# Batched VectorE operations for the token places, rows and weights of eight small experts in a perceiver layer

## The chip, the core and the metric

The kernel runs on one core of a Trainium2 chip, in float32 throughout its large products. A core has five engines that run their own instruction queues: PE (TensorE, matrix products), DVE (VectorE), ACT (ScalarE), POOL (GpSimd) and SP (SyncE, which here only issues transfers). The metric is device time in microseconds (us), the median of three executions: 758.45 us before the change (758.18 to 758.95).

## What is computed

One layer of a perceiver over 256 tokens of width 512: cross-attention with a sigmoid over a context of 25,088 rows, causal self-attention, and a mixture of experts. Only the last part matters here:

```python
logits = x @ gate_w                          # 256 tokens, 64 experts
w, idx = top_k(softmax(logits), 8)           # w divided by its sum
pos = (place of the token among those that chose the same expert)
slot = minimum(pos, CAPACITY)                # CAPACITY = 256
buf[e_flat, slot] = x[tok]
gu_e = einsum('ech,ehf->ecf', buf, expert_gate_up_w)
act = silu(gu_e[..., :I]) * gu_e[..., I:]
out_e = einsum('eci,eih->ech', act, expert_down_w)
y = out_e[e_flat, slot] * w_flat[:, None]
return y.sum(over the 8 choices) + shared    # shared: a gated expert that every token uses
```

## The kernel before

Up to about 560 us the kernel computes the cross-attention (lines L336 to L593 in the profile's largest groups), then the self-attention. The expert part begins near 611 us. The shared expert is cut in four pieces, `("s", 0)` to `("s", 3)`. The 64 experts are sorted by how many tokens chose them. The seven largest, `("e", 0)` to `("e", 6)`, are computed for all 256 tokens. The next eight (numbers 7 to 14, `FEW` = 8) are small: for these only the tokens that chose them are gathered, into four rounds of 128 slots. A round holds quarters of 32 slots: round 0 has three quarters of expert 9 and one of expert 10, round 1 one quarter each of experts 11 to 14, round 2 three of expert 8 and one of expert 7, round 3 four of expert 7.

The function `run` (L1474) goes through the pieces `("s", 0)` to `("s", 3)`. For each it calls `gate_up`: a product on PE (L1263), a sigmoid on ACT (L1289), two products on VectorE (L1290, L1291), and a scaling `weigh` on VectorE (L1300), after which VectorE adds four sums `s_s` (L1364) and POOL four sums `t_s` (L1364) for a down product in seven block products (`seven`, L1380). After piece i it calls the step of the dictionary `between`: `counted` after piece 0, `load_first` after 1, `ranked_tokens` after 2, `seated` after 3. The seven products of a piece stand on PE's queue behind the gate and up products of the next piece.

`ranked_tokens` brings the routing weights into the sorted order (`wso`) and finds for each token its `rank` among those that chose each of the eight small experts, -1 where it did not (L1638, L1646). `rank` has 128 partitions (tokens) by 2 halves of the tokens by 8 experts. `seated` then

- writes `places_of`, one 0/1 matrix of tokens by slots for each half and round: for each of the two halves of the tokens and each of nine ranges of slots one VectorE comparison of the slot numbers `slot_sb` with one column of `rank` (L1663, 18 operations of 32, 96 or 128 columns),
- multiplies it on PE with the token numbers (`token`, L1673, 8 small products), turns the result into integers (`token_i`, L1681), and has POOL issue four indirect gathers of the tokens' rows (`few_rows`, L1683),
- computes for each small expert the row from which a token will later fetch its result (`row`, L1697 and L1700), and the weight that it fetches with (`fetched_w`, L1703): three operations of 128x2 elements for each of eight experts, 24 in all, after a `memset` of `row` (L1692),
- turns `row` into integers (`row_of_token`, L1706), and clears the weights of fetched tokens in `wso` (L1709, eight operations).

The VectorE and POOL instructions of `seated` carry no fixed place; a scheduler puts them among those of `gate_up`. In the program before, 13 of the comparisons stand ahead of L1290 of piece 3 on VectorE's queue, the other five comparisons and 25 of the small operations between L1290 and L1291, and L1706 and one more between L1291 and L1300. On PE the order is: gate and up products of piece 3, the seven products of piece 2, the eight `token` products, the seven products of piece 3, then the first large expert.

The row `fn` of normalised tokens, from which the gathers read, is written by VectorE at L282 in two halves, transposed by PE (L298), and stored by POOL (`rows_of_tokens`, L1181).

Of the kernel before, what the change touches and what calls it, by code (L numbers as in the profile page):

```python
# [9 lines left out]
F32 = mybir.dt.float32  # L10
BF16 = mybir.dt.bfloat16
AF = mybir.ActivationFunctionType
ALU = mybir.AluOpType
AX = mybir.AxisListType

P = 128
# [6 lines left out]
def tile_perceiver_layer(  # L23
# [25 lines left out]
    nc = tc.nc  # L49
# [10 lines left out]
    NT = T // P  # L60
# [175 lines left out]
    slot_sb = const.tile([P, T], F32, tag="slot", name="slot_sb")  # L236
# [284 lines left out]
    for i in range(2):  # L521
        t = cpool.tile([P, NT_SUMS, WIDTH + 2], F32, tag=f"T{i}", name=f"T_{i}", bufs=1)
# [94 lines left out]
    for t in range(NT):  # L617
        for c in range(ND):
            at = (c % 2) * T + t * P
# [82 lines left out]
    for line in RESULTS.strip().splitlines():  # L702
        to, x_, op, y_ = line.split()
        a_, b_, o_ = result(x_), result(y_), result(to)
        n = widths[to] = min(widths[x_], widths[y_])
        assert to not in ("c01", "c11") or n == WIDTH
        if to[0] == "c" and to[2] != "1":
            n = WIDTH - 2
# [74 lines left out]
    def banks(name):  # L783
        return pairs.tile([P, 2, 512], F32, tag="two", name=name)
# [7 lines left out]
    def bank(name):  # L792
        turns[1] += 1
        return apart(name) if turns[1] % 4 == 0 else among_three(name)
# [3 lines left out]
    for t in range(NT):  # L798
# [14 lines left out]
    WHOLE = 7  # L813
    QUARTER = P // 4
# [7 lines left out]
    NR = len(ROUNDS)  # L822

    STORED = ((0,), (1,), (2, 3))
    QUARTERS = {
        k: sum(n for part in ROUNDS for of, n in part if of == k)
        for k in sorted({of for part in ROUNDS for of, _ in part})
    }
    FEW = len(QUARTERS)
# [363 lines left out]
    few = ctx.enter_context(tc.tile_pool(name="few", bufs=1))  # L1193
# [197 lines left out]
    def add_seven():  # L1391
# [18 lines left out]
    first, second = (  # L1410
        [pair[:, half, :] for half in range(2)]
        for pair in (banks("ph_first"), banks("ph_second"))
    )
# [146 lines left out]
    places_of = few.tile([P, NT, NR, P], BF16, tag="places_of", name="places_of")  # L1560
# [6 lines left out]
    fetched_w = few.tile([P, NT, FEW], F32, tag="fetched_w", name="fetched_w")  # L1567
# [40 lines left out]
    def slots_of_round(r):  # L1608

        first = 0  # L1610
        for k, n in ROUNDS[r]:
            ahead = sum(m for part in ROUNDS[:r] for of, m in part if of == k) * QUARTER
            yield k, first, n * QUARTER, ahead
            first += n * QUARTER

    rank = few.tile([P, NT, FEW], F32, tag="rank", name="rank")
    w = wso[:, :, WHOLE : WHOLE + FEW]

# [26 lines left out]
        )  # L1645
        nc.vector.tensor_scalar(rank, rank, 1.0, None, ALU.subtract)  # L1646

    def first_row(k):
        for rounds in STORED:
            for i, r in enumerate(rounds):  # L1650
                for of, first, _, ahead in slots_of_round(r):
                    if of == k:
                        assert ahead == 0
                        return i * P + first

    def seated():


        for t in range(NT):
            for r in range(NR):  # L1660
                for k, first, n, ahead in slots_of_round(r):
                    i = k - WHOLE
                    nc.vector.tensor_scalar(  # L1663
                        places_of[:, t, r, first : first + n],
                        slot_sb[:, ahead : ahead + n],
                        rank[:, t, i : i + 1],
                        None,
                        ALU.is_equal,
                    )
        token = bank("token")[:, 0:NR]  # L1670
        for r in range(NR):
            for t in range(NT):
                nc.tensor.matmul(  # L1673
                    token[:, r : r + 1],
                    lhsT=places_of[:, t, r, :],
                    rhs=tokens_sb[:, t : t + 1],
                    start=(t == 0),
                    stop=(t == NT - 1),
                )
        token_i = few.tile([P, NR], mybir.dt.int32, tag="token_i", name="token_i")  # L1680
        nc.vector.tensor_copy(token_i, token)  # L1681
        for r in range(NR):
            nc.gpsimd.indirect_dma_start(  # L1683
                out=few_rows[:, r, :],
                out_offset=None,
                in_=rows_of_tokens[:, :],
                in_offset=bass.IndirectOffsetOnAxis(ap=token_i[:, r : r + 1], axis=0),
            )


        row = few.tile([P, NT, FEW], F32, tag="row", name="row")
        nc.vector.memset(row, 0.0)  # L1692
        for k, n in QUARTERS.items():
                i = k - WHOLE
                first = first_row(k)
                n *= QUARTER
                nc.vector.tensor_scalar(  # L1697
                    row[:, :, i], rank[:, :, i], 0.0, n - 1.0, ALU.max, ALU.min
                )
                nc.vector.tensor_scalar(  # L1700
                    row[:, :, i], row[:, :, i], float(first), None, ALU.add
                )
                nc.vector.scalar_tensor_tensor(  # L1703
                    fetched_w[:, :, i], rank[:, :, i], float(n), w[:, :, i], ALU.is_lt, ALU.mult
                )
        nc.vector.tensor_copy(row_of_token, row)  # L1706
        for k, n in QUARTERS.items():
            i = k - WHOLE
            nc.vector.scalar_tensor_tensor(  # L1709
                w[:, :, i], rank[:, :, i], float(n * QUARTER), w[:, :, i], ALU.is_ge, ALU.mult  # L1710
            )

    run(
        [("s", k) for k in range(NS)],
# [259 lines left out]
```

## Time and profile before

| | before |
|---|---|
| median of three executions | 758.45 us |
| profiled execution, whole | 758.16 us |
| its span | 756.0 us |
| PE busy | 748.9 us (99%) |
| VectorE busy | 574.9 us (76%) |
| POOL busy | 208.9 us (28%) |
| L1663, 18 operations | duration 224 to 808 ns, median 229 |
| L1697, L1700, L1703, L1709, 32 operations | 145 to 155 ns each |
| granted TensorE clock | 1.0 |

The span is the time from the first to the last recorded work of the profiled execution; 2.2 us of its whole time lie around it. In the profile, an answer on the chain of waits goes back from the last instruction to what released it, and shows which engine held up the end at each moment. A timeline shows the instructions of an engine with start, length, and what ended the idle time before them. Consecutive VectorE operations overlap in these records: an operation of 150 ns may follow another after 70 ns, so the distance from start to start, and not the duration, says what an operation costs in a row of them.

### The profile page before, as it was taken

Reading aid. Unit: us, or ns where it says so; the run is one execution under the profiler, and the core shown is the slowest. Engines: PE = TensorE matmul, PEld = TensorE weight load, DVE = VectorE, ACT = ScalarE, POOL = GpSimd, SP = SyncE. Lnnn points to the kernel's source line nnn. Section 1 sums busy time; section 2 is a strip of 40 time slices with the busy share of each in tenths; the row PEclk is TensorE's granted clock in tenths of the full one; section 3 lists DMA queues with packets and bytes.
Section 4 is the critical chain, followed back from the end, with each engine's and each line's share of the span. In section 5 each row is a group of like instructions: output and inputs, shape, how many; then the busy total and the mean of one; then the engine's idle time right before and its main releaser. Section 6 shows DMA issues by size and latency. Waiting matters only on the chain.

```text
span 756.0 us, 12474 instructions
## 1 busy us (share of the span) xinstructions
PE 748.9 (99%) x4046; PEld 614.3 (81%) x4046; DVE 574.9 (76%) x1682; ACT 200.7 (27%) x484; POOL 208.9 (28%) x378
## 2 busy tenths in 40 slices
PE   8999999999999999999999999999999999999998
PEld 6888888888888888888888888888977578876775
DVE  6988887887888788788888878878677569542465
ACT  4222222222222222222222222222244530001110
POOL 3222222232232222223222222322213305440461
PEclk9999999999999999999999999999999999999999
DMA  9999989997887887787788778774060018998552
GB/s 248 262 234 253 276 217 304 251 214 196 206 189 176 216 192 172 201 200 183 187 210 189 170 211 196 177 198 95 1 219 33 2 38 283 388 339 320 174 176 71
DMA packets 156147, 148.64 MB, mean 197 GB/s; under 512 B 8310, under 2 KB 113923, under 8 KB 156080
## 3 DMA queue, kind: packets, MB, share of 16 engines
q1 hardware_dynamic: 153168, 140.28, 71.3%
q0 software_dynamic: 2240, 7.02, 2.8%
q8 instruction: 33, 0.54, 0.3%
q10 hardware_dynamic: 672, 0.52, 0.2%
q14 instruction: 34, 0.28, 0.1%
HBM read 145.63 MB, written 2.16 MB: 195 GB/s over the span
## 4 chain that ended last, share of the span: by engine, by line
PE 97%; DVE 2%; DMA 0%; ACT 0%; issue 0%
PE xacc L593 38%; PE pk L372 22%; PE pz L392 11%; PE ph_e L1263 7%; PE seven L1380 3%; PE pa L914 2%; PE pw L983 2%; PE ph_few L1745 2%; PE ph_s L1263 1%; PE po_few L1776 1%; PE ph_first L1263 1%; PE ph_second L1263 1%; PE pd_last L1448 1%; PE ptp L1065 1%; PE ps L1009 1%; PE py L757 1%
## 5 line engine op out<-in xcount | busy, mean ns | idle before, releaser
L593 PE MATMUL xacc<-T,S 128*128 128x172 f32 (+2 forms) x912 | 185.5, 308 | 0.0
L372 PE MATMUL pk<-cT,wkT_sb 128*128 128x384 f32 x512 | 175.5, 486 | 0.0
L593 PEld LDWEIGHTS xacc<-T,S 128*128 128x128 f32 x912 | 152.6, 190 | 20.1
L372 PEld LDWEIGHTS pk<-cT,wkT_sb 128*128 128x128 f32 x512 | 97.1, 190 | 54.4
L560 POOL TENSOR_TENSOR T<-ctx 128x172 f32<-128x172 f32 x65 | 32.3, 496 | 386.1 <-PE xacc L593 375.5
L336 DVE STREAM_TRANSPOSE cT<-quarters 128x1536 f32<-128x1536 f32 x64 | 113.2, 1769 | 0.5 <-issue 0.5
L560 DVE TENSOR_TENSOR T<-ctx 128x172 f32<-128x172 f32 (+1 forms) x262 | 113.4, 433 | 0.0
L560 DVE TENSOR_TENSOR S<-zT 128x128 f32<-128x128 f32 x196 | 56.2, 287 | 70.9 <-ACT zT L401 70.9
L392 PE MATMUL pz<-qT,kT 128*128 128x256 f32 x392 | 106.1, 379 | 0.0
L401 ACT ACTIVATE zT<-pz 128x256 f32<-128x256 f32 (+1 forms) x131 | 64.2, 490 | 113.7 <-PE pz L392 113.7
L593 PE MATMUL xacc<-T,zT 128*128 128x173 f32 (+1 forms) x396 | 89.9, 308 | 0.0
L593 PE MATMUL xacc<-ctx,S 128*128 128x172 f32 x392 | 78.5, 309 | 0.0
L383 ACT ACTIVATE kT<-pk,bk 128x384 f32<-128x384 f32 (+2 forms) x68 | 38.5, 568 | 146.9 <-PE pk L372 146.9
L570 ACT COPY T<-ctx 128x170 f32<-128x170 f32 (+1 forms) x130 | 43.2, 334 | 124.9 <-PE xacc L593 123.5
L560 DVE TENSOR_TENSOR S<-zT,S 128x128 f32<-128x128 f32 x325 | 76.0, 283 | 0.0
L560 POOL TENSOR_TENSOR T<-ctx,T 128x170 f32<-128x170 f32 (+1 forms) x130 | 72.4, 576 | 0.0
L560 DVE TENSOR_TENSOR T<-ctx,T 128x172 f32<-128x172 f32 x195 | 65.4, 360 | 8.2 <-PE xacc L593 1.5
L392 PEld LDWEIGHTS pz<-qT,kT 128*128 128x128 f32 x392 | 68.5, 190 | 3.8 <-ACT kT L383 0.2
L593 PEld LDWEIGHTS xacc<-T,zT 128*128 128x128 f32 x396 | 66.4, 190 | 0.3
L593 PEld LDWEIGHTS xacc<-ctx,S 128*128 128x128 f32 x392 | 62.8, 190 | 0.1
L593 PE MATMUL xacc<-ctx,zT 128*128 128x170 f32 (+1 forms) x264 | 59.5, 307 | 0.0
L1263 PE MATMUL ph_e<-fT,gu 128*128 128x256 f32 x224 | 50.3, 381 | 0.0
(308 smaller groups left out, 793.9 us busy)
## 6 DMA issues: line engine op xcount, KB each, us to landing
ctx<-in_context SPq DMA_DIRECT2D x65, 768.0 KB, 5.3
quarters<-in_context SPq DMA_DIRECT2D x256, 192.0 KB, 6.5
gu<-in_e_gate_up SPq DMA_DIRECT2D x12, 1024.0 KB, 7.9
gu_s<-in_s_gate_up SPq DMA_DIRECT2D x8, 512.0 KB, 5.9
dn<-in_e_down SPq DMA_DIRECT2D x7, 512.0 KB, 6.6
a_wqT<-in_a_wqT SPq DMA_DIRECT2D x4, 512.0 KB, 10.0
a_wout<-in_a_woutT SPq DMA_DIRECT2D x1, 2048.0 KB, 11.6
dn_s<-in_s_down SPq DMA_DIRECT2D x4, 512.0 KB, 8.0
```

Source lines behind the costliest of these rows:

```text
L336: in_turn(nc.vector.transpose(new_turned(g), q.rearrange("p b (c r) -> p c b r", r=R)))
L372: nc.tensor.matmul(pk, lhsT=w[:, c, :], rhs=cT[:, c, 0 : n // R, :].rearrange("p b r -> p (b r)"), start=(c == 0), stop=(c == ND - 1),)
L383: in_turn(nc.scalar.activation(kT[:, lo:hi], pk[:, lo:hi], AF.Identity, bias=bk_sb))
L392: nc.tensor.matmul(pz[:, i * T : (i + 1) * T], lhsT=kT[:, at : at + P], rhs=qT, start=True, stop=True,)
L401: nc.scalar.activation(zT[:, blocks[0] : blocks[-1] + 1, :].rearrange("p j t -> p (j t)"), pz[:, 0 : len(blocks) * T], AF.Sigmoid, scale=1 ...
L560: in_turn(f(o_, a_, b_))
L570: in_turn(nc.scalar.copy(named[to][:, 0:n], named[x_][:, 0:n]))
L593: nc.tensor.matmul(banks_of_products[i][:, cols], lhsT=named[lhs], rhs=named[rhs][:, 0:n],  start=i not in opened, stop=(g == G - 1 and last),
L914: nc.tensor.matmul(pa[:, 0 : hi - lo], lhsT=a_wqT_sb[:, c, e * P : (e + 1) * P], rhs=anT[:, c, lo:hi], start=(c == 0), stop=(c == ND - 1),)
L983: nc.tensor.matmul(pw[t], lhsT=oT[:, e, t * P : (t + 1) * P], rhs=a_wout_sb[:, e, :], start=(e == 0), stop=(e == NE - 1),)
L1263: nc.tensor.matmul(ph[:, f * T + lo : f * T + hi], lhsT=gu[:, c, col : col + P], rhs=fT[:, c, lo:hi], start=(c == 0), stop=(c == ND - 1),)
L1380: nc.tensor.matmul(product_of_seven(nm), lhsT=block(n, hT, dn, s_, t_, lhs), rhs=block(n, hT, dn, s_, t_, rhs),  start=(n == SEVEN[0] and ...
```

## The change

The 18 comparisons become eight. A list `places` holds the ranges of slots, where neighbouring one-quarter experts with neighbouring numbers are one entry: for each half of the tokens one comparison of 96 columns (expert 9), one `tensor_tensor` of 160 columns for experts 10 to 14 together (`slot_sb` and `rank` both broadcast), one of 96 (expert 8) and one of 160 (expert 7, over the border of two rounds). The 24 operations for `row` and `fetched_w`, the `memset` and the eight for `wso` become five operations over all eight experts; with the cast they are six. Three constants for each expert are taken from a new small tile `numbers` (128 partitions by 3 by 8), which POOL fills with 24 `memset` operations of 128x1 elements.

In the built program the instructions stand thus. On POOL the 24 memsets lie between the two stores of `rows_of_tokens` (L1181), and the first of them waits for the last reads of the memory that `numbers` takes over (VectorE's L1173 for the second half of the tokens, and PE's L983). On VectorE all eight comparisons, then the two operations of `row` and the cast, stand ahead of L1290 of piece 3; the last three operations stand between L1290 and L1291; none are between L1291 and L1300. `token_i` stands behind the four sums `s_s` of piece 3. The order on PE, ACT and SP is as before. The tiles of the same memory pool that follow `numbers` lie 96 bytes further on.

```diff
+    place_of, places = {}, []
+    for r in range(NR):
+        for k, within, n, ahead in slots_of_round(r):
+            at = r * P + within - ahead
+            assert place_of.setdefault(k, at) == at
+            if ahead:
+                continue
+            if places and QUARTERS[k] == 1:
+                k0, many, at0 = places[-1]
+                if QUARTERS[k0] == 1 and (k, at) == (k0 + many, at0 + many * QUARTER):
+                    places[-1] = (k0, many + 1, at0)
+                    continue
+            places.append((k, 1, at))
+
+    numbers = few.tile([P, 3, FEW], F32, tag="numbers", name="numbers")
+    for k, n in QUARTERS.items():
+        row_0 = min(rs[0] for rs in STORED if place_of[k] // P in rs) * P
+        for i, value in enumerate((n * QUARTER, n * QUARTER - 1, place_of[k] - row_0)):
+            nc.gpsimd.memset(numbers[:, i, k - WHOLE : k - WHOLE + 1], float(value))
+
+    def of_expert(i):
+        return numbers[:, i, :].unsqueeze(1).to_broadcast([P, NT, FEW])
...
     def seated():
+        flat = places_of.rearrange("p t r s -> p t (r s)")
         for t in range(NT):
-            for r in range(NR):
-                for k, first, n, ahead in slots_of_round(r):
-                    i = k - WHOLE
+            for k, many, at in places:
+                n = QUARTERS[k] * QUARTER
+                i = k - WHOLE
+                if many == 1:
                     nc.vector.tensor_scalar(
-                        places_of[:, t, r, first : first + n],
-                        slot_sb[:, ahead : ahead + n],
+                        flat[:, t, at : at + n],
+                        slot_sb[:, 0:n],
                         rank[:, t, i : i + 1],
                         None,
                         ALU.is_equal,
                     )
+                else:
+                    nc.vector.tensor_tensor(
+                        flat[:, t, at : at + many * n].rearrange("p (e s) -> p e s", e=many),
+                        slot_sb[:, 0:n].unsqueeze(1).to_broadcast([P, many, n]),
+                        rank[:, t, i : i + many].unsqueeze(2).to_broadcast([P, many, n]),
+                        ALU.is_equal,
+                    )
...
-        nc.vector.memset(row, 0.0)
-        for k, n in QUARTERS.items():
-                i = k - WHOLE
-                first = first_row(k)
-                n *= QUARTER
-                nc.vector.tensor_scalar(
-                    row[:, :, i], rank[:, :, i], 0.0, n - 1.0, ALU.max, ALU.min
-                )
-                nc.vector.tensor_scalar(
-                    row[:, :, i], row[:, :, i], float(first), None, ALU.add
-                )
-                nc.vector.scalar_tensor_tensor(
-                    fetched_w[:, :, i], rank[:, :, i], float(n), w[:, :, i], ALU.is_lt, ALU.mult
-                )
+        nc.vector.scalar_tensor_tensor(row, rank, 0.0, of_expert(1), ALU.max, ALU.min)
+        nc.vector.tensor_add(row, row, of_expert(2))
         nc.vector.tensor_copy(row_of_token, row)
-        for k, n in QUARTERS.items():
-            i = k - WHOLE
-            nc.vector.scalar_tensor_tensor(
-                w[:, :, i], rank[:, :, i], float(n * QUARTER), w[:, :, i], ALU.is_ge, ALU.mult
-            )
+        nc.vector.tensor_tensor(row, rank, of_expert(0), ALU.is_lt)
+        nc.vector.tensor_mul(fetched_w, row, w)
+        nc.vector.tensor_sub(w, w, fetched_w)
```

More of the change, by code (lines that the diff above doesn't have):

```diff
@@ L1646, in ranked_tokens @@
         nc.vector.tensor_scalar(rank, rank, 1.0, None, ALU.subtract)
[L1648 to L1654, printed above, removed]
     def seated():
+        flat = places_of.rearrange("p t r s -> p t (r s)")
         for t in range(NT):
-            for r in range(NR):
-                for k, first, n, ahead in slots_of_round(r):
-                    i = k - WHOLE
+            for k, many, at in places:
+                n = QUARTERS[k] * QUARTER
+                i = k - WHOLE
+                if many == 1:
                     nc.vector.tensor_scalar(
-                        places_of[:, t, r, first : first + n],
-                        slot_sb[:, ahead : ahead + n],
+                        flat[:, t, at : at + n],
+                        slot_sb[:, 0:n],
                         rank[:, t, i : i + 1],
                         None,
+                        ALU.is_equal,
[5 more added lines that the diff above has]
+                        rank[:, t, i : i + many].unsqueeze(2).to_broadcast([P, many, n]),
                         ALU.is_equal,
```

## The prediction

> **What bounds the kernel now.** I read the page first: PE is busy 748.9 us of 756.0, and the chain that ended last lies on PE for 97%. So VectorE's many operations cost nothing except where PE stands still for them, and the first question is where it does. The answer on PE's waits, over the whole span, has four rows (who waited for whom, total us, times, longest):
>
> ```profile
> PE pi L210 <- DVE idle_sb L97: 1.5, 1, 1.5
> PE seven L1380 <- DVE hT_s L1300: 0.7, 1, 0.7
> PE pt_xn L621 <- DVE xn L610: 0.6, 1, 0.6
> PE pa L914 <- ACT aq L928: 0.2, 1, 0.2
> ```
>
> Only the second lies in the changed stage. The chain of waits between 636 and 660 us (start, us, what) shows how it comes about:
>
> ```profile
> 644.34 0.07 PE pn L1631 x3
> ...
> 644.43 0.19 DVE rank L1638
> ...
> 644.64 0.66 DVE rank L1646
> ...
> 645.32 3.73 DVE places_of L1663 x13
> 649.05 0.59 DVE hT_s L1290
> 649.65 0.81 DVE places_of L1663 x5
> ...
> 652.22 0.60 DVE hT_s L1291
> 652.82 0.08 DVE row_of_token L1706
> 652.90 0.07 DVE wso L1709
> 652.97 0.61 DVE hT_s L1300
> 653.58 0.04 issue
> 653.62 3.29 PE seven L1380 x14
> ```
>
> From 644.43 to 653.62 the chain is VectorE's alone; it is 9 us long, but PE works beside nearly all of it. A table of busy time for that stretch (window, its length, PE, PEld, DVE, ACT and POOL busy, clock, DMA share, GB/s) says how much:
>
> ```profile
> 644.60:653.62 9.02, 8.28 (x46) 7.14 (x45) 8.95 (x52) 0.60 (x1) 2.76 (x4) 1.00 1.05 386
> ```
>
> VectorE is full (8.95 of 9.02) and PE misses 9.02 - 8.28 = **0.74 us**. That is the whole prize of this stage, whatever number of VectorE operations goes away: PE's timeline has the eight token products start at 652.54 and end 0.34 later, at 652.88, and the next seven products at 653.62.
>
> **The eight comparisons.** Before, 18 of them take 3.73 + 0.81 = 4.54 us of the chain. Part of this is POOL: its four sums `t_s` run at 644.53, 645.34, 646.02 and 646.71, the last until 647.44, and in that time VectorE gets only one operation through for each of POOL's (one of 96 columns from 645.32 lasts 0.81, one of 32 from 646.05 lasts 0.73, where the median is 229 ns). After: three operations (96, 160, 96) pass in that time as three passed before, and five are left at 647.4. Ten operations and the step to L1290 took 647.39 to 648.97 before, 0.158 each; the widest forms cost more, so I take 0.2 each: 648.4. The `tensor_tensor` of 160 columns is not in the trace of before. Its lower end is one comparison's 0.16; above, `s_s<-hT_s` of 128x128 from SBUF stands 0.20 apart (two in 0.48, the second lasting 0.28), and 32 more columns add about 0.03: 0.23. If it is held for a whole sum of POOL it costs 0.73, twice: 1.5. I take 0.23, the row of the same operation.
>
> **The six operations on 128x16.** Before, 25 small ones stood between L1290 and L1291 (650.38 to 652.14, 1.76 us, 0.07 apart because they alternate between experts) and two more between L1291 and L1300 (0.15). After, each operation reads what the one before it wrote. The row for that is L1638 to L1646, 644.43 to 644.64: 0.21 apart. Three of them before L1290: 648.4 + 0.63 = 649.0. L1290 takes 0.60: 649.6. Three more: 650.3. L1291 (its product on PE ends at 649.68, so nothing holds it) 0.60, L1300 0.61 and its 0.04: **651.5**. PE is through with the token products at 652.88. So VectorE comes some 1.3 us ahead of PE, and the gap closes even if one `tensor_tensor` is held for a full sum of POOL. What is late next is PE itself.
>
> **The rest of the edit.** The memset of `row` (L1692, 72 ns at 615.13) goes; VectorE waits 0.20 for ACT right behind it, which hides it: nothing. `token_i` stood at 654.73 and can now follow the token products near 653.1, so POOL's four gathers begin some 1.6 us earlier. They were through by 667, and PE reads `few_rows` at 673.4: nothing. The eight clearings of `wso` are read by nothing before the end: nothing. The sums `t_s` of piece 3 end at 647.44 and PE needs them at 654: a delay by the wider VectorE operations is covered sixfold.
>
> After 653.62 PE waits for no one by the table of waits, so 0.74 us at this place should reach the end in full, if no transfer is late. The DMA engines are full from 644 to 673 (share 1.05), so I looked for the nearest arrival. The weights of the second large expert are issued at 644.42 and take 7.9 us in the median, 10.9 at most: 655.3, read at about 664. Those of the third: 654.25 and 665.2, read at 674.0. Eight us of cover against 0.74. SP's later issues wait for PE to free buffers and move with it.
>
> **POOL's 24 memsets** are the one thing added. They wait for VectorE's L1173, which ends at 614.09, and stand ahead of POOL's second store of `rows_of_tokens` (616.66), whose rows are gathered 38 us later: as a delay of POOL this is nothing. But VectorE is then on the path to `fn`, and PE has almost no cover there:
>
> ```profile
> 0.28 0.10 POOL L1959 MEMSET const-float32-1.0<- 128x1 f32 x1
> 0.31 0.11 POOL L1959 MEMSET const-bfloat16-1.0<- 128x1 bf16 x1
> ...
> 615.64 0.72 DVE L282 TENSOR_SCALAR fn<-x,mv_f,rs_f 128x256 f32<-128x256 f32 x2
> ...
> 616.43 0.25 PEld L298 LDWEIGHTS pt_fn_behind<-ident,fn 128*128 128x128 f32 x2
> ```
>
> `fn` ends at 616.36 and PE loads it at 616.43: cover 0.07. The row for a memset of 128x1 on POOL is the start of the kernel: 0.10 to 0.12 long, but 0.03 apart. By it 24 take 24 x 0.03 + 0.1 = 0.8 us, so even with 0.3 us until POOL starts they are over by 615.2, before `fn` at 615.64. Only L1625 (614.73) lies among them, and can be held for one memset, 0.12 - 0.07 = 0.05 at PE.
>
> Against this stands the Trainium skill, "SBUF — State Buffer", section "Who interferes with whom": VectorE in a mode that uses two ports and GpSimd lock each other out for a whole instruction. `fn` looks like such an operation (128x512 at L282 takes 547 ns and 128x256 takes 402, 0.57 ns an element, against 1.04 for a product that reads PSUM, 691 and 424). If I set the memsets end to end at 0.10 each, they run to about 616.6 and, with the lock never given back between them, `fn` starts 0.96 late: 0.89 at PE, and the change would cost 0.15. The trace shows the lock changing hands after each of POOL's sums, so I take the row: **0.05**.
>
> **Sum:** -0.74 + 0.05 = -0.69 us. Against the profiled execution's own 758.16 that is 757.47; the median of the runs, 758.45, is 0.29 above that execution, and from it the sum gives 757.76. I say **757.7**, nearer the median, since three executions stand behind it. About 0.2%, 1.5 us, is what can be told from no change here, so this is a gain too small to call.
>
> **Rivals.**
>
> *The gap moves instead of closing.* PE comes 0.74 earlier to something that is then late: the gate weights, or the end, where VectorE waits 0.84 for `few_rows` at 748.49. Time: no change, 758.2 to 758.5. For it: the DMA engines are full in this stage. Against: 8 us of cover at the nearest weights, and the tail's gathers follow from PE's own products. The wide comparisons held by POOL lead here as well, if they eat 1.3 us. 0.12.
>
> *The memsets stop VectorE: slower.* One mechanism: POOL's train of memsets keeps the port from 614.1 and `fn` waits for its end. It decides from the point where the train outlasts 615.64 by 0.07 + 0.74, 616.45, or 98 ns from start to start. POOL's smallest copies, 1x1, last 174 to 246 ns; at 246 the train runs 5.9 us, to 620.0, `fn` is 4.36 late, PE 4.29, and the sum is +3.55: 762.0 from the median. Against it: 0.03 apart in the trace, and the alternation at 645 to 647. 0.08.
>
> *More than the gap is won.* PE would have to lose other idle time, but in the stretch from 653.62 to 756 it misses 3.55 us, nearly all of it after its last product ends near 752.5. Nothing there to win. 0.03, with 756.5 for it.
>
> *The change does not do what it says:* the built program has the eight and six operations; only their lengths are open.
>
> **Chances and range.** Forecast 0.77, gap moved 0.12, slower 0.08, more 0.03. Only the last two leave the 1.5 us: faster 0.03, same 0.89, slower 0.08. The range goes from 757.0 (0.83, PEld's own wait, and the spread of the runs below the median, 0.3, with a little over) to 758.8 (no change, or the 0.15 of memsets end to end, and a run's spread); the 762 is left out.
>
> **What would show it.** Right: no row for `seven` among PE's waits; L1300 of piece 3 ends near 651.5; products of piece 3 begin at 652.9 on a clock that is otherwise that of before; POOL's memsets stand 0.03 apart and are over by 615.2. Wrong: a PE wait for `fn` near 616.4 (the memsets), a comparison of 160 columns longer than 0.8 us (POOL's hold), or a new wait for a transfer after 653.

## The result and the profile after

The changed kernel takes 757.0 us (median of 18 executions, 756.78 to 757.63). The kernel before, on the same chip, takes 758.2 (18 executions, 757.93 to 758.95). The ratio is 0.9984, with a 95% interval from 0.9977 to 0.9991: a gain of 1.2 us, where 0.7 was forecast and called too small to tell.

| us | before | after |
|---|---|---|
| median of 18 executions | 758.2 | 757.0 |
| profiled execution, whole | 758.16 | 757.02 |
| its span | 756.0 | 755.2 |
| what lies around the span | 2.16 | 1.82 |
| VectorE busy | 574.9 | 571.6 |

The last three rows already say much: VectorE lost 3.3 us of work and the span 0.8, and a third of a microsecond of the gain is not in the span at all.

PE's waits over the whole span of the changed kernel (who waited for whom, total us, times, longest):

```profile
PE pi L210 <- DVE idle_sb L97: 1.5, 1, 1.5
PE pa L914 <- ACT aq L928: 0.2, 1, 0.2
```

The row for `seven` is gone, as forecast. So is that for `pt_xn`, but it lies in the first ten us, which the change doesn't touch: there `x_sb` landed 0.36 us later in this execution than in the profiled one of before, and four other products of PE (`ptc`) came later too (they end at 7.17, not 6.06) and stand where PE waited before. By the time of the changed stage every instruction is 0.16 us later (`ph_second` before `pt_fn` starts at 615.88 before and at 616.04 after), and I take 0.16 off where I compare clock times below.

The chain of waits of the changed kernel no longer touches VectorE in this stage (start, us, what):

```profile
644.55 5.29 PE ph_s L1263 x24
649.84 3.02 PE seven L1380 x14
652.86 0.18 PE token L1697 x8
653.04 3.13 PE seven L1380 x14
656.17 3.88 PE ph_e L1263 x18
```

The second `seven` row is 3.13 long; before, the same 14 products stood in the chain with 3.29. And busy time in the stretch that the prediction used (window, its length, PE, PEld, DVE, ACT, POOL, clock, DMA share, GB/s):

```profile
644.60:653.62 9.02, 9.02 (x49) 7.88 (x49) 8.00 (x24) 0.60 (x1) 3.00 (x5) 1.00 1.05 387
```

PE is now full (9.02 of 9.02). VectorE has 24 instructions there in place of 52, and is busy for 8.00 us in place of 8.95, since it goes on with later work.

VectorE's timeline after the change (start, length, instruction) shows how far ahead it now is:

```profile
646.22 0.88 DVE L1688 TENSOR_TENSOR places_of<-slot_sb,rank 128x160 bf16<-128x160 f32 x1
...
648.06 0.31 DVE L1688 TENSOR_TENSOR places_of<-slot_sb,rank 128x160 bf16<-128x160 f32 x1
648.29 0.47 DVE L1680 TENSOR_SCALAR places_of<-slot_sb,rank 128x96 bf16<-128x96 f32 x2
...
651.07 0.69 DVE L1300 TENSOR_TENSOR hT_s<-hT_s,wqT 128x512 f32<-128x512 f32 x1
```

The same operation on 160 columns stands 0.80 from the next instruction while POOL sums and 0.23 from it when POOL is done. L1300 ends at 651.76, 1.3 us before the token products end on PE (653.04).

### The profile page after: what moved, and what is told of

It reads as the page before. It is cut to its first block, busy times and chain, and to the rows that moved or that the text cites. A ratio compares the mean times of both kernels' runs of the same rounds, so it can differ in the third digit from the quotient of the medians.

```text
span 755.2 us, 12461 instructions
## 1 busy us (share of the span) xinstructions
PE 749.6 (99%) x4046; PEld 614.8 (81%) x4046; DVE 571.6 (76%) x1644; ACT 200.9 (27%) x484; POOL 209.2 (28%) x402
## 3 DMA queue, kind: packets, MB, share of 16 engines
HBM read 145.63 MB, written 2.16 MB: 196 GB/s over the span
## 4 chain that ended last, share of the span: by engine, by line
PE 99%; DVE 1%; ACT 0%; issue 0%
PE xacc L593 38%; PE pk L372 22%; PE pz L392 11%; PE ph_e L1263 7%; PE seven L1380 4%; PE pa L914 2%; PE ph_s L1263 2%; PE pw L983 2%; PE ph_few L1755 2%; PE po_few L1786 1%; PE ph_first L1263 1%; PE ph_second L1263 1%; PE pd_last L1448 1%; PE ptp L1065 1%; PE ps L1009 1%; PE py L757 1%
```

## The experiments

Each was measured beside the kernel before on the same chip. Three quantities are read from each. The *stage* goes, in the chain of waits, from the first `seven` product of piece 0 to the end of those of piece 3: 635.45 to 656.91 = 21.46 us before, 635.61 to 656.17 = **20.56** after, so the stage gave 0.90 and not 0.74. The *span* is the median over the executions. *Outside* is the median of each execution's time less its span: 2.2 us before, 1.78 after (1.73 to 1.90, against 2.13 to 2.29 in 45 executions of before).

### The kernel before again

It shows what two copies of one program differ by.

> The kernel before, unchanged, timed run for run with its span. Theory A (the whole gain is PE's gap ahead of the seven products of piece 3, with what PE loses when it starts again after it; the remaining 0.3 us are the profiled execution's own scatter): span 756.0 in the median or up to 0.3 more, and time less span the same 1.8 us as in the runs of the changed kernel. Theory B (a part of the gain, some 0.35 us, lies outside the span: the profiled executions show 758.16 less 756.0 = 2.16 before and 757.02 less 755.2 = 1.82 after): time less span 2.1 to 2.2 in nearly every run.

Measured: 758.53 us (13 executions) beside 758.29 (45), ratio 1.0002 [0.9994, 1.001]; stage 21.46, span 756.3, outside 2.21. So 1.2 us is well above what this measurement makes of nothing.

### Each half alone

The first kernel has only the comparisons batched, the second only rows and weights (with `numbers` and its memsets):

```diff
# e1_comparisons: before, with the eight comparisons
-            for r in range(NR):
-                for k, first, n, ahead in slots_of_round(r):
+            for k, many, at in places:
...
# e2_rows: before, with the six operations on all experts
-        nc.vector.memset(row, 0.0)
-        for k, n in QUARTERS.items():
...
+        nc.vector.scalar_tensor_tensor(row, rank, 0.0, of_expert(1), ALU.max, ALU.min)
+        nc.vector.tensor_add(row, row, of_expert(2))
```

> Only the comparisons batched (eight instead of 18), rows and weights as before. Theory A: VectorE saves about 1.3 us ahead of L1300 of piece 3, but now has all eight clearings of the weights ahead of L1291 (0.4 us more), so L1300 ends near 652.8 and PE's gap of 0.74 closes nearly or quite: 757.0 to 757.3, nearly all of the whole change's gain. If the two halves of the change add up instead (theory C: the gain follows the count of VectorE operations, 10 of 37 removed), about 0.3 us, 757.9. Theory B by instructions: the part outside the span shrinks with the program's length, so by about a quarter of 0.35.

> Only rows and weights batched (six instead of 33, with the 24 memsets on POOL and the new tile), the 18 comparisons as before. Theory A: from 649.57 five comparisons (0.81), six dependent operations (1.25), L1291 (0.6), L1300 (0.65): L1300 ends near 652.9, PE's gap closes to within 0.1: 757.0 to 757.3, so that this and the run with the comparisons alone each give nearly the whole gain. Theory C: 27 of 37 operations, about 0.9 us, 757.3.

Measured: 757.15 us, ratio 0.9985 [0.9978, 0.9992], stage 20.73, span 755.3, outside 1.84 for the comparisons; 757.30 us, ratio 0.9987 [0.9979, 0.9995], stage 20.86, span 755.5, outside 1.80 for the rows. Each half gives nearly all of the gain, and together they give hardly more: the gap of PE caps what the stage can yield. But neither stage is 20.56. (The profiled execution of the rows alone has a span of 757.2, since PE waited 1.5 us for VectorE in the cross-attention; its stage is not touched by that.) PE's timeline of the kernel with comparisons alone shows why (the last line is of VectorE's):

```profile
652.13 0.59 PE L1380 MATMUL seven<-dn_s,s_s 128*128 128x256 f32 x2
652.56 0.34 PE L1696 MATMUL token<-tokens_sb,places_of 128*128 128x1 bf16 x8
652.91 1.13 PE L1380 MATMUL seven<-dn_s,hT_s 128*128 128x256 f32 x4
...
652.16 0.69 DVE L1300 TENSOR_TENSOR hT_s<-hT_s,wqT 128x512 f32<-128x512 f32 x1
```

There is no wait to be seen, since the token products end at 652.90 and `seven` starts at 652.91; yet the stage is 0.17 longer than with the whole change. The first two lines tell the rest: the token products start at 652.56, 0.16 *before* the `seven` ahead of them end (652.13 + 0.59 = 652.72). Groups of products overlap by about 0.16 in these records, and here the next group didn't: L1300 ends only at 652.85, so it still held `seven` back, from a start 0.20 behind that of the token products, as after the whole change (652.70 and 652.90), to one 0.35 behind. (The expectations further on call this 0.16 TensorE's restart.) In the kernel with the rows alone, `seven` starts 0.13 after the token products end, and 0.30 is lost.

### The memory shift alone

The tile `numbers` moves the tiles behind it by 96 bytes. This kernel is the one before with that tile, unused.

```diff
+    few.tile([P, 3, FEW], F32, tag="numbers", name="numbers")
     rank = few.tile(
```

> The kernel before with the new tile of 96 bytes allocated at its place but neither written nor read: all later tiles of the pool lie 96 bytes further on, as in the changed kernel, and no instruction is added. Theory A: no change, 758.2. Theory D (the shift, which puts the gathered experts' weights on 64-byte borders, gives the part of the gain that the gap doesn't): 757.8 to 757.9, with shorter transfers or products after 674 us, or 0.35 us less outside the span.

Measured: 758.30 us beside 758.29, ratio 1.0 [0.9992, 1.0008], stage 21.43, outside 2.25. The shift is worth nothing.

### Moved instead of batched

Nothing is batched here. The small operations for rows and weights are made to depend on `token_i`, so that they run after 653 us, where PE no longer waits for VectorE; five comparisons stay between L1290 and L1291.

```diff
-        nc.vector.memset(row, 0.0)
+        for to in (row, fetched_w):
+            nc.vector.tensor_copy(
+                to.rearrange("p t i -> p (t i)"), token_i[:, 0:1].to_broadcast([P, NT * FEW])
+            )
```

> The kernel before with all its small operations for rows and weights, but behind the integer token numbers (the first two read these), so that they run in VectorE's idle time after 653 us: nothing is batched, VectorE's program is as long as before (2045). Theory A with E: L1300 of piece 3 ends near 651.7, PE's gap closes, the span falls by 0.9 to 755.2, and the 2.2 outside stay: 757.4. If the gain came from fewer operations as such: no change, 758.3. If all of the gain belongs to the gap: 757.1 with 1.8 outside.

Measured: 757.20 us, ratio 0.9985 [0.9978, 0.9991], stage 20.56, span 755.3, outside 1.88. VectorE's timeline of this kernel:

```profile
649.90 0.89 DVE L1663 TENSOR_SCALAR places_of<-slot_sb,rank 128x32 bf16<-128x32 f32 x5
...
651.43 0.69 DVE L1300 TENSOR_TENSOR hT_s<-hT_s,wqT 128x512 f32<-128x512 f32 x1
```

L1300 ends at 652.12, before the token products end at 653.23. So the stage's gain is a matter of what stands ahead of L1300, not of how many operations there are: the same number of operations, later, gives the same.

### The gap opened again

Three, and in a second kernel six, unread products of 128x512 are put ahead of L1291 of piece 3 in the changed kernel.

```diff
+        if n == ("s", 3):
+            for _ in range(3):
+                nc.vector.tensor_mul(more_rooms[:, 0, :], hf, hf)
         nc.vector.tensor_mul(hf, pu, hf)
```

> The changed kernel with three products of 128x512 that nobody reads added on VectorE between the two products of piece 3 (L1290 and L1291), about 0.6 us each, 1.85 together. In the changed kernel L1300 ends 1.1 us before PE is through with the token products, so PE should stand still for 0.7 us again. Theory A: the span grows by these 0.7 and by what the restart costs, 0.16 (the seven products took 3.29 us behind the gap and 3.13 without it): 756.1, and 757.9 to 758.0 in time, with 1.8 outside. Without a cost of the restart: 757.7.

> The changed kernel with six unread products of 128 x 512 between L1290 and L1291 of the small expert's third piece, twice those of the run with three (wait 0.6, stage 21.35). If each product is 0.68 to 0.70 us and TensorE's restart costs a fixed sum, the wait is 0.6 + 3 x 0.6 = 2.4 to 2.7 us, the seven products behind it take 3.29 us again (0.16 over those without a wait), and the stage is 20.56 + wait + 0.16 = 23.2 to 23.4 us, the span about 757.8 to 758.0 and the time 759.6 to 759.9. If the restart grows with the length of the wait, the seven products take more than 3.4 us. If the work in between were covered elsewhere later, the time would stay under 758.5.

Measured with three: 757.69 us, ratio 0.9993 [0.9985, 1.0002], span 755.9, outside 1.79, stage 21.35. PE's waits have a row for `seven` again:

```profile
PE seven L1383 <- DVE hT_s L1303: 0.6, 1, 0.6
```

Measured with six: 759.89 us (7 executions, 759.47 to 761.28), ratio 1.0017 [0.999, 1.0045], span 758.0, outside 1.88. PE's timeline:

```profile
652.50 0.34 PE L1700 MATMUL token<-tokens_sb,places_of 128*128 128x1 bf16 x8
652.71 0.68 PE L1263 MATMUL ph_e<-fT,gu 128*128 128x256 f32 x2
655.68 1.13 PE L1383 MATMUL seven<-dn_s,hT_s 128*128 128x256 f32 x4 [2.30 <-DVE hT_s L1303]
```

Two products of the first large expert now stand ahead of `seven`; elsewhere in this trace such products stand 0.215 apart. The stage is 655.68 + 3.29 - 635.41 = 23.56, less 2 x 0.215 for work done early: 23.13, 2.57 more than 20.56 for a wait of 2.30.

Set beside each other, idle time of PE ahead of `seven` and what the stage lost against 20.56:

| kernel | idle | stage lost |
|---|---|---|
| after | none, groups overlap | 0 |
| e1_comparisons | 0.01 | 0.17 |
| e2_rows | 0.13 | 0.30 |
| e6_late3 | 0.62 | 0.79 |
| before | 0.74 | 0.90 |
| e6_late6 | 2.30 | 2.57 |

Except in the last row the loss is the idle time plus 0.16 to 0.17, whatever the length of the wait. It is the overlap of one group with the next, which a group that starts late doesn't have. In the last row 0.27 comes on top of the idle time: the 0.16, and 0.1 more where the order on PE differs. The two `ph_e` behind the token products last 0.68, where two products of this form last 0.59 elsewhere, and `seven` behind the wait needs 0.97 to its second group (655.68 to 656.65), where it needs 0.86 behind other large products. In the other kernels only `seven` pays this 0.1, with a wait or without; here both groups do.

### What lies outside the span

The stage explains 0.9 of a gain of 1.2 or a little more. The rest is outside the span, and all kernels so far fell into two classes there: 2.2 us for before, its copy and the one with the memory shift, 1.8 for the others. The first guess was the length of VectorE's program, counted in the compiled instructions of its one long block: 2043 in the three with 2.2, 2033, 2016 and 2006 in the comparisons alone, the rows alone and the whole change. The next two kernels are the changed one with 38 and with 24 copies of `token_i` into an unused column, after 653 us:

```diff
+        spare = few.tile([P, 1], F32, tag="spare", name="spare")
+        for _ in range(38):
+            nc.vector.tensor_copy(spare, token_i[:, 0:1])
```

> The changed kernel with 38 copies of one number added on VectorE behind the integer token numbers, in its idle time after 653 us, so that VectorE's program is as long as before (2044 instructions in its long block against 2043 before and 2006 changed) while the gap stays closed. The four kernels so far show 2.22 us outside the span for the two whose VectorE program has 2043, 1.78 to 1.84 for those with 2033, 2016 and 2006. Theory E (a length of VectorE's program beyond some point between 2033 and 2043 costs 0.4 us outside the span): span 755.2 as in the changed kernel, 2.2 outside, 757.4. Theory F (what is outside the span follows from what the operations do, or from PE's gap): 1.8 outside, 757.0.

> The same with 24 copies: 2030 instructions. Theory E: below the point, so 1.8 outside the span and 757.0. If the part outside grows evenly with the number of instructions instead: 0.42 * 24/37 = 0.27 more, 2.05 outside, 757.3.

Measured: with 38 copies (2044 instructions) 756.96 us, ratio 0.9982 [0.9974, 0.999], and outside 1.77; with 24 (2030) 757.09 us, ratio 0.9985 [0.9978, 0.9992], and 1.79; both stages 20.56. So it is not enough to be longer than 2033; the moved kernel, with 2045, says the same by its 1.88 where 2.2 was expected. What remained was that only exactly 2043 was dear. Two kernels test it from both sides, the kernel before with one copy more (2044) and the changed one with 37 copies (2043):

> The kernel before with one more VectorE copy (token_i into a spare tile of one column, at 653 us, where VectorE has no hurry), so that VectorE's program has 2044 instructions in its long block in place of 2043. What lies outside the span is 2.2 us in the three kernels with exactly 2043 (before, e0, e3) and 1.8 us in all others. Theory F (the program's last instructions stand badly at exactly this length): outside 1.8, span still 756.1, so the time is about 757.9. Rival (what lies outside comes from what is computed in the stage of the routing, or from the wait of TensorE there, not from the length): outside 2.2, time 758.3. The stage from the start of seven to the start of ph_e stays at 21.4 to 21.5 us by both, with TensorE's wait of 0.7 us.

> The changed kernel with 37 copies of token_i into a spare tile at 653 us, so that VectorE's long block has exactly 2043 instructions, the number of the kernel before. Theory F (the length alone): outside the span 2.2 us, span 755.2, so the time is about 757.4. Rival (not the length): outside 1.8, time 757.0. The stage stays at 20.56 us by both.

Measured: the kernel before with one copy more takes 757.74 us where the kernel before beside it takes 758.21, ratio 0.9995 [0.9987, 1.0003], span 755.9: as whole times the two can't be told apart. But its outside is 1.84 (13 executions, 1.74 to 1.93), beside 2.20 (35 executions, 2.11 to 2.27), and these ranges don't touch. Its gap on PE is still there, by PE's timeline:

```profile
653.46 1.13 PE L1380 MATMUL seven<-dn_s,hT_s 128*128 128x256 f32 x4 [0.64 <-DVE hT_s L1300]
```

The changed kernel with 2043 takes 757.36 us, ratio 0.9988 [0.9982, 0.9995], stage 20.56, span 755.2, outside 2.16 (2.11 to 2.28). With one copy more it had 1.77, and the two programs differ in that copy alone. The length decides, with or without the gap. The last run takes one copy away:

> The changed kernel with 36 copies in place of 37: VectorE's long block has 2042 instructions, one fewer than in the run that showed 2.16 us outside the span, two fewer than in the ones that showed 1.77 and 1.84. If exactly one length is bad (the program's end standing at one place): outside the span 1.8 us, time 757.0. If a few neighbouring lengths are bad, with 2043 the last of them: outside 2.2, time 757.4. Span 755.2 and the stage 20.56 us by both.

Measured: 757.31 us, ratio 0.9984 [0.9978, 0.9991], span 755.2, outside 2.14 (2.07 to 2.26). So at least two neighbouring lengths are dear:

| instructions in VectorE's long block | kernels | outside, us |
|---|---|---|
| 2006 to 2033 | after, e1, e2, e5, both e6 | 1.78 to 1.88 |
| 2042 | e10 | 2.14 |
| 2043 | before, e0, e3, e9 | 2.16 to 2.27 |
| 2044, 2045 | e4, e8, e7 | 1.77 to 1.88 |

What the chip does at these lengths stays open. The trace has no row for it, since it lies before the first or after the last recorded work; lengths from 2034 to 2041 were not tried.

## Why the prediction was wrong, step by step

**What bounds the stage: right.** The wait of `seven` for L1300 was PE's only one there, and closing it was the gain inside the span. Taking the wait away by moving work gives what the change gives, and either half alone gives nearly that; putting it back takes it away again.

**The prize of the stage: mis-sized.** The prediction said of the gap of 0.74 us: "That is the whole prize of this stage". The stage gave 0.90. The 0.74 was counted from the end of the token products to the start of `seven`; but PE's groups start before the group ahead of them ends, and that overlap came back too. It stood in the profile of before, on PE's timeline (the last two lines are of after):

```profile
652.11 0.59 PE L1380 MATMUL seven<-dn_s,s_s 128*128 128x256 f32 x2
652.54 0.34 PE L1673 MATMUL token<-tokens_sb,places_of 128*128 128x1 bf16 x8
653.62 1.13 PE L1380 MATMUL seven<-dn_s,hT_s 128*128 128x256 f32 x4 [0.74 <-DVE hT_s L1300]
...
652.70 0.34 PE L1697 MATMUL token<-tokens_sb,places_of 128*128 128x1 bf16 x8
652.90 1.11 PE L1380 MATMUL seven<-dn_s,hT_s 128*128 128x256 f32 x4
```

The first two groups of before overlap by 652.11 + 0.59 - 652.54 = 0.16, the token products and `seven` don't; after the change these two overlap by 0.14. From start to start, `seven` follows the token products by 1.08 before (652.54 to 653.62) and by 0.20 after, and these 0.88 are the gain of the stage but for 0.02. The prediction's sign "products of piece 3 begin at 652.9" has the same fault: on the clock of before they begin at 652.74. Its range did name a longer wait, the 0.83 of PE's weight load, but the sum took 0.74. The 3.29 in the chain, longer than the 3.13 that the same 14 products take without a wait, is the same 0.16 seen from behind.

**The sum: a term was missing.** "Against the profiled execution's own 758.16 that is 757.47" took the 2.2 us around the span as a constant. They fell by 0.4, for a reason that has to do with the number of VectorE's instructions alone. The rival "more than the gap is won" was given 0.03 with "Nothing there to win", which speaks of the time inside the span only; it is what happened, for these two reasons. With both terms corrected the sum is -0.90 - 0.42 = -1.3 us; the medians differ by 1.2. The starting point was off as well: 18 executions put the kernel before at 758.2, where three had given 758.45, so 0.25 of the distance from the forecast 757.7 to the measured 757.0 lies there.

**The memsets: right in the choice, 0.05 too dear.** POOL's timeline after the change:

```profile
614.40 0.85 POOL L1634 MEMSET numbers<- 128x1 f32 x24 [3.63 <-DVE x L1173]
```

24 of them end at 615.25, forecast 615.2, and `fn` starts at 615.80, 0.16 later than before, which is the shift of the start. The cost was nothing, and the rival that POOL's train stops VectorE falls: the lock of the Trainium skill's page "SBUF — State Buffer", section "Who interferes with whom", would have made `fn` 0.96 late with memsets end to end at 0.10 each and the lock never given back between them. But they stood 0.03 apart, and the train was over before `fn` was due, so no run here shows what the lock would have done to it.

**VectorE's own times: right at the end, by luck in part.** L1300 ends at 651.76, 651.60 on the clock of before; forecast 651.5. The three operations of the rows ahead of L1290 were forecast to end at 649.0; L1290 starts at 649.25, or 649.09. Behind it two misses cancel, which is luck: L1291 follows L1290 by 1.10 where the sum had 1.23, and L1300 follows L1291 by 0.72 where it had 0.60. Of the comparisons of 160 columns the second, free of POOL, took the 0.23 of the nearest row. The first lasted 0.88 beside POOL's sums. "Longer than 0.8 us" stood among the signs of being wrong, and the sign misled: the comparison stood where a narrow one of before had been held for 0.73, so it cost little more than that one.

**What is late next: right.** No transfer was late. From 656 us to the end the two executions keep the same distance of 0.74, which is the stage's 0.90 less the start's 0.16.

**The chances: wrong.** A gain under 1.5 us was put down as not to be told from no change. With 18 executions on each side the interval of the ratio ended 0.09% short of 1.

## What to carry to other kernels

Count what a wait of PE costs from start to start of the groups around it, or take the length of the group behind it where it doesn't wait: the idle time in the wait's row leaves out the overlap that a late group loses, 0.16 us here. Ask which wait the removed work stood ahead of, not how much work goes away: of 3.3 us of VectorE time removed only the part ahead of one L1300 paid, and half of the change paid nearly as much, only moving work behind it just as much. Where gains are below a microsecond, split the measured time into the span and what lies around it for each execution, and compare these apart, since a program can gain or lose 0.4 us around the span by one instruction more.

## What was not expected of the hardware

- The time around the span depends on the exact number of instructions in VectorE's program: 2.14 to 2.27 us at 2042 and 2043, 1.77 to 1.88 at 2044 and 2045 and at those tried from 2006 to 2033. One unused copy took this time from 2.20 to 1.84 in the kernel before.
- 24 memsets of 128x1 on POOL went through in 0.85 us, 0.03 apart, and VectorE beside them kept its times (`ahead`, L1625 before and L1648 after, took 0.21 in both).
- While POOL summed tiles, one VectorE comparison went through for each of POOL's sums, whatever its width: 0.81 us for 96 columns, 0.88 for 160, against 0.31 for 160 columns alone. A wide operation costs little more than a narrow one in such a stretch.
